# A transformer decoder layer on one core: the order of the first loads, masks and transposes

## The chip, the cores and the metric

The kernel runs on one core of a Trainium2 chip. The core has a matrix engine (PE), a vector engine (DVE), a scalar engine for activation functions (ACT), a general engine (POOL) and a queue engine (SP), which work side by side and meet through semaphores. Transfers between the chip's memory and the on-chip buffers are issued by SP, ACT and POOL and carried by 16 DMA engines that all three share. The metric is the device time of one execution in microseconds, lower is better.

## The reference

The computation is one post-norm decoder layer on x of 16 x 256 tokens with 256 features, in float32: a "quantum" self-attention, a differential cross-attention over a context, and a mixture of four experts, each followed by a layer norm. Only the beginning of the first attention matters here:

```python
Q = (x @ wq + bq).reshape(Bn, Sn, Hn, hd)      # 16 heads of 16 features; K with wk, bk, V with wv, bv
def prep(t):
    h1 = jnp.tanh(jnp.einsum('bshd,do->bsho', t, w1) + b1)     # 16 -> 256 for each head
    return jnp.einsum('bsho,on->bshn', h1, w2) + b2            # 256 -> 16
qp, kp = (prep(Q), prep(K))
q1 = jnp.einsum('bshn,nm->bshm', qc, Hc)        # qc, kc: complex pairs of the 16; Hc: the 8 x 8 hadamard
...                                             # rotations by rot, squared norms qq and kk
attn = jax.nn.softmax(s / s, axis=2)            # s = qq * kk
out = jnp.einsum('bijh,bjhd->bihd', attn, V).reshape(Bn, Sn, Dn)
return out @ wo + bo
```

Since everything from w2 to the Hadamard matrix is linear, the kernel multiplies the second layer's weights (and b2) by the Hadamard matrix once, at the start.

## The kernel before, in words

Tokens are worked in 8 pairs of sequences, 512 tokens each, q = 0 to 7. For a pair, `turn_x` (line 801) transposes two halves of features of x on PE, four 128 x 128 blocks into one PSUM bank, and DVE copies the bank out as xT. `project` (811) multiplies xT with wk or wq into `pq`; DVE adds the bias into qT. `hidden(t)` (830) is one of 16 steps of a pair: four matmuls of 32 rows (`ph`), two heads' first layers, with w1 taken from a tile `w1p` that holds w1 eight times, once per head, masked for even and odd heads; ACT takes tanh of the two results (`h`). `outer` (845) multiplies `h` with the second layer's weights `w2p` into `pe`. All `mm` calls share line 119 in the profile.

The first lines of `first_attention` (777) issue the loads: wk on SP, then on ACT's queue the eight copies of w1 (783), bk, b1 and rot; wq, wv, wo on SP; bq on ACT; x of the pairs 1 to 7 on SP. Before them x of pair 0 was issued on SP. After the function definitions come, in program order, the two `turn_x` of pair 0 and its first `project` (1001 to 1003), the head masks on POOL (`mask8`), their sum `mpar` on DVE (1010), the two products that mask `w1p` (1013), further masks on POOL, and then the loads of w2T, b2 and the 8 x 8 Hadamard matrix on ACT (1043 to 1053). That matrix is put twice on the diagonal of `hb1`, a 16 x 16 tile that DVE clears first; DVE also clears `w2p`. `second_layer` (1056), planned for step 0, multiplies w2T by hb1 (`pw`), copies the result into `w2p`, and multiplies b2 by an expanded copy of hb1 (`hbd`) into the bias `b2c`.

Each engine runs its instructions in program order: for PE, ACT and DVE the order is that of the code (`ORDERED`, line 27), which the plan's steps write out (line 1125: `hidden(t)` first, then planned work, then `outer` of the step before). A DMA is issued at its place in the order of the engine that issues it. SP's and ACT's transfers use eight completion counters in rotation, in the order in which both queues are laid out; a transfer whose counter was used before is issued only after that earlier transfer has landed. PSUM banks for `ptx`, `pq` and `pw` come from `bank` (798), a pool tagged `sm` with one buffer, so that each use waits until the one before was read; `pe` has a bank of its own in the pool `pse`, not used before the first `outer`.

Of the kernel before, what the change touches and what calls it, by code (L numbers as in the profile page):

```python
# [9 lines left out]
F32 = mybir.dt.float32  # L10
# [5 lines left out]
P = 128  # L16
B, S, D = 16, 256, 256
# [46 lines left out]
def bc(ap, axis, n):  # L64

    shape = list(ap.shape)
    return ap.unsqueeze(axis).to_broadcast(shape[:axis] + [n] + shape[axis:])
# [3 lines left out]
def decoder_kernel(ctx: ExitStack, tc: tile.TileContext, a: dict, out: bass.AP):  # L71
    nc = tc.nc
    PE, DVE, ACT, POOL, SP = nc.tensor, nc.vector, nc.scalar, nc.gpsimd, nc.sync
# [17 lines left out]
    def mat(pool, key, n, eng=SP):  # L91

        k = a[key].shape[0]
        t = pool.tile([P, k // P, n], F32, tag=key, name=key)
        eng.dma_start(out=t, in_=a[key].rearrange("(c p) f -> p c f", p=P))
        return t

    def col(pool, key, eng=SP):

        n = a[key].shape[0]  # L100
        t = pool.tile([P, n // P], F32, tag=key, name=key)
        eng.dma_start(out=t, in_=a[key].rearrange("(c p) -> p c", p=P))
        return t
# [14 lines left out]
    def mm(out_, lhsT, rhs, start=True, stop=True):  # L118
        PE.matmul(out=out_, lhsT=lhsT, rhs=rhs, start=start, stop=stop)  # L119
# [648 lines left out]
    hd = heads.enter_context(tc.tile_pool(name="hd", bufs=1))  # L768
    ps = heads.enter_context(tc.tile_pool(name="psA", bufs=1, space=PSUM))
    pse = heads.enter_context(tc.tile_pool(name="psAe", bufs=1, space=PSUM))  # L770
    psb = heads.enter_context(tc.tile_pool(name="psAb", bufs=3, space=PSUM))
    wH = folds.enter_context(tc.tile_pool(name="wH", bufs=1, side="right"))
# [4 lines left out]
    def first_attention():  # L777

        plan = Plan()
        wk = mat(hd, "L0_attn_wk", D)  # L780
        w1p = hd.tile([P, 2, D], F32, tag="w1p", name="w1p")
        for k in range(8):
            ACT.dma_start(out=w1p[16 * k:16 * k + 16, 1, :], in_=a["L0_attn_w1"])
        bk, b1 = (col(hd, f"L0_attn_{n}", ACT) for n in ("bk", "b1"))
        rot = wH.tile([H, NQ, 3], F32, tag="rot", name="rot")
        ACT.dma_start(out=rot, in_=a["L0_attn_rot"])
        wq, wv = (mat(hd, f"L0_attn_{n}", D) for n in ("wq", "wv"))
# [10 lines left out]
        def bank(name):  # L798
            return banks[0].tile([P, 512], F32, tag="sm", name=name)

        def turn_x(q, c):
            xq = xs[:, q * CPB:(q + 1) * CPB, :]
            xT = xTs[q, c] = hd.tile([P, TB], F32, tag="xT", name="xT", bufs=4)
            pt = bank("ptx")
            for n in range(CPB):
                PE.transpose(pt[:, n * P:(n + 1) * P], xq[:, n, c * P:(c + 1) * P], ident)
            DVE.tensor_copy(xT, pt)
            if c == 1:
                POOL.tensor_tensor(xq, xq, bc(bo, 1, CPB), ALU.add)

        def project(q, side, cc):
            w, bias = ((wk, bk), (wq, bq))[side]
            qT = qTs[q, side, cc] = hd.tile([P, TB], F32, tag="qT", name=f"qT{q}{side}", bufs=2)
            pq = bank("pq")
            for c in range(2):
                mm(pq, w[:, c, cc * P:(cc + 1) * P], xTs[q, c], c == 0, c == 1)
            DVE.tensor_scalar(qT, pq, bias[:, cc:cc + 1], None, ALU.add)
# [180 lines left out]
            DVE.tensor_tensor(xv, pf.rearrange("p (i d) -> p i d", i=2), xv, ALU.add)  # L998
            plan.later(1, norm, n0)

        for c in range(2):
            turn_x(0, c)
        project(0, 0, 0)

        mask8 = hd.tile([P, 8], F32, tag="mask8", name="mask8")
        POOL.memset(mask8, 1.0)
        POOL.affine_select(mask8, mask8, [[-16, 8]], ALU.is_ge, 0.0, base=0, channel_multiplier=1)
# [3 lines left out]

        for par in range(2):
            DVE.tensor_scalar(w1p[:, par, :], w1p[:, 1, :], mpar[:, par:par + 1], None, ALU.mult)

        b16 = tl.tile([P, H], F32, tag="b16", name="b16")
        POOL.memset(b16, 1.0)
# [23 lines left out]
                DVE.tensor_copy(selc[:, cc, 8 * cc:8 * cc + 8], b8)  # L1040


        w2T = wH.tile([16, D], F32, tag="w2T", name="w2T")
        ACT.dma_start(out=w2T, in_=a["L0_attn_w2T"])
        b2 = wH.tile([16, 1], F32, tag="b2", name="b2")
        ACT.dma_start(out=b2, in_=a["L0_attn_b2"].unsqueeze(1))
        hbd = wH.tile([16, 8, 16], F32, tag="hbd", name="hbd")
        hb1 = wH.tile([16, 16], F32, tag="hb1", name="hb1")
        DVE.memset(hb1, 0.0)
        for k in range(2):  # L1050
            ACT.dma_start(out=hb1[8 * k:8 * k + 8, 8 * k:8 * k + 8], in_=a["L0_attn_hadamard"])
        w2p = hd.tile([P, 2, 2, 32], F32, tag="w2p", name="w2p")
        DVE.memset(w2p, 0.0)
        b2c = hd.tile([P, 1], F32, tag="b2c", name="b2c")

        def second_layer():
# [54 lines left out]
        for q in range(NPAIR):  # L1111
            s0 = 16 * q
            for c in range(2):
                if q:
                    plan.job(s0 - 6, s0 - 4 + c, turn_x, q, c)
            for side in range(2):
                for cc in range(2):
                    f = s0 + 8 * side + 4 * cc
                    if f:
                        plan.job(f - 3, f - 1, project, q, side, cc)  # L1120
            for half in range(2):
                plan.job(*((s0 + 15, s0 + 24 + half) if q < NPAIR - 1 else (LAST - 2, 0)), values, q, half)
# [362 lines left out]
    with ExitStack() as own:  # L1485
        own.enter_context(tc.manual_schedule(engines=ORDERED))
        planA, stepA, fold = first_attention()
        xw, xb, tri, mw, mb, rb = ffn_small()
        zero = tl.tile([P, P], F32, tag="zero", name="zero")
# [100 lines left out]
```

## Time and profile before

| | us |
|---|---|
| median of 3 runs (lowest, highest) | 1847.62 (1845.48, 1850.51) |
| profiled execution | 1848.87 |
| its span, first to last instruction | 1846.9 |
| PE busy in 0 to 28 us | 12.08 |
| PE busy in 28 to 60 us | 30.23 |
| PE busy in 60 to 100 us | 40.00 |

A line of the profile names the engine, the source line, the operation, and its output and inputs with the program's tile names, from which digits are dropped: `hb` is hb1, `b` is b2 or b16 according to its line, and `L_attn_b` of line 102 is b1. "ACTq" and "SPq" stand for the time in which an engine issues a transfer. The brackets give how long the engine had been idle and what ended that. Where an engine spends its time in issuing transfers, which isn't counted as busy, a wait is put down to the transfer that came last.

### The profile page before, as it was taken

What the parts mean: (1) busy time and instruction counts of PE and PEld (TensorE: products, weight loads), DVE (VectorE), ACT (ScalarE), POOL (GpSimd) and SP (SyncE); (2) the same over time, 40 slices, a digit from 0 to 9 for tenths busy, and PEclk for the clock granted to TensorE, in tenths of its full rate; (3) what the DMA queues carried; (4) which work ended last, traced back from release to release, by engine and by line L of the source; (5) the groups of instructions that cost most, each with busy time, mean ns of one, the idle gap of its engine ahead of it and who ended that gap; (6) DMA issues with size and microseconds to landing.
All of it is one profiled execution on the core that took longest, in us unless ns stands there. A gap on an engine that the chain in (4) does not pass through costs nothing. (4 is left out here: it accounts for less than half of the span.)

```text
span 1846.9 us, 32370 instructions
## 1 busy us (share of the span) xinstructions
PE 1682.0 (91%) x12254; PEld 960.4 (52%) x12254; DVE 960.4 (52%) x2033; ACT 942.6 (51%) x1368; POOL 536.5 (29%) x1235
## 2 busy tenths in 40 slices
PE   6999999999999999999999999997987999899743
PEld 2343434343444656656565655564664758566533
DVE  1225656655556876777766666672213334121565
ACT  3547777777777576665655556554322222231210
POOL 5001313212313333344634343445320110131331
PEclk9999999999999999999999999898998999899876
DMA  9912111212112200000101000011333001221322
GB/s 258 297 50 70 65 59 59 69 59 93 58 59 98 65 14 14 3 25 14 37 2 36 2 25 2 25 37 47 102 103 109 20 28 48 82 75 39 106 64 81
DMA packets 117771, 115.34 MB, mean 62 GB/s; under 512 B 7776, under 2 KB 111408, under 8 KB 117584
## 3 DMA queue, kind: packets, MB, share of 16 engines
q1 hardware_dynamic: 108560, 93.08, 15.8%
q0 software_dynamic: 7824, 19.65, 3.6%
q8 instruction: 114, 1.87, 0.4%
q14 instruction: 73, 0.60, 0.1%
q10 hardware_dynamic: 1200, 0.15, 0.1%
HBM read 73.79 MB, written 38.54 MB: 61 GB/s over the span
## 5 line engine op out<-in xcount | busy, mean ns | idle before, releaser
L1307 DVE TENSOR_REDUCE mpad<-p 128x4 f32<-128x1024 f32 x256 | 311.3, 1218 | 142.3 <-PE p L119 141.4
L1313 ACT ACTIVATE e<-p 128x512 f32<-128x512 f32 x512 | 276.7, 596 | 175.5 <-PE p L119 173.7
L841 ACT ACTIVATE h<-ph,L_attn_b 128x1024 f32<-128x1024 f32 x256 | 271.3, 1112 | 160.9 <-PE ph L119 160.9
L119 PE MATMUL p<-qp,kT 32*128 32x256 f32 x2048 | 315.3, 410 | 18.2 <-DVE o L1360 13.3
L119 PE MATMUL p<-kT,qp 32*128 32x256 f32 x2048 | 314.1, 409 | 1.5 <-DVE mpad L1307 1.5
L119 PEld LDWEIGHTS p<-kT,qp 32*128 32x128 f32 x2048 | 193.7, 188 | 91.0 <-issue 49.7
L119 PEld LDWEIGHTS p<-qp,kT 32*128 32x128 f32 x2048 | 207.9, 190 | 31.7 <-issue 25.6
L119 PE MATMUL ph<-qT,w1p 32*128 32x512 f32 x1024 | 152.3, 652 | 3.1 <-ACT h L841 1.8
L935 DVE TENSOR_TENSOR z<-rqb,ra 128x1024 f32<-128x1024 f32 x120 | 151.5, 1265 | 3.7 <-DMA rqb<-rqd 1.7
L119 PE MATMUL pe<-h,w2p 128*32 128x512 f32 x1024 | 138.2, 612 | 1.6 <-DVE enc L858 0.9
L119 PE MATMUL pob<-e,vaug 128*32 128x512 f32 x1024 | 128.3, 620 | 0.0
L942 ACT ACTIVATE z<-z 128x1024 f32<-128x1024 f32 x120 | 127.1, 1060 | 1.3 <-DVE z L935 0.9
L628 POOL DMA_INDIRECT ya<-xlist,place x64 | 62.8, 981 | 205.0 <-DVE xs L638 86.7
L159 POOL TENSOR_SCALAR ln_ve<-ln_mv 128x2 f32<-128x2 f32 x32 | 7.2, 225 | 351.3 <-DVE ln_mv L157 350.5
L119 PE MATMUL pw<-xeT,L_ffn_sw_w 128*128 128x512 f32 (+1 forms) x256 | 85.8, 496 | 12.8 <-DVE xeT L478 12.8
L163 POOL TENSOR_SCALAR xs<-xs,ln_mv,rs_y 128x256 f32<-128x256 f32 x64 | 83.8, 1314 | 3.4
L478 ACT ACT_TABLE_LOAD x17 | 21.8, 1283 | 113.7 <-PE pt L477 113.3
L119 PE MATMUL po<-z,vaug 128*32 128x256 f32 x1024 | 72.8, 389 | 6.7 <-DVE ra L895 1.6
L119 PEld LDWEIGHTS pw<-xeT,L_ffn_sw_w 128*128 128x128 f32 x256 | 50.0, 196 | 47.1 <-issue 28.7
L404 POOL DMA_INDIRECT xlist<-xs,place x64 | 62.7, 980 | 37.1 <-DVE place L401 19.7
L119 PEld LDWEIGHTS ph<-qT,w1p 32*128 32x128 f32 x1024 | 42.5, 184 | 53.8 <-issue 42.0
L1339 ACT COPY ovTb<-pob 128x512 f32<-128x512 f32 x64 | 37.5, 585 | 58.2 <-PE pob L119 58.2
(349 smaller groups left out, 2598.1 us busy)
## 6 DMA issues: line engine op xcount, KB each, us to landing
rqb<-rqd SPq DMA_DIRECT2D x64, 512.0 KB
xlist<-zero SPq DMA_DIRECT2D x16, 1024.0 KB
xe<-xlist SPq DMA_DIRECT2D x21, 512.0 KB
xlist<-ye SPq DMA_DIRECT2D x14, 512.0 KB
xs<-in_x SPq DMA_DIRECT2D x8, 512.0 KB
cx<-in_ctx SPq DMA_DIRECT2D x8, 512.0 KB
qp<-st SPq DMA_DIRECT2D x256, 2.0 KB
out<-xs SPq DMA_DIRECT2D x8, 512.0 KB
```

Of the source, the lines that this page charges most:

```text
L119: PE.matmul(out=out_, lhsT=lhsT, rhs=rhs, start=start, stop=stop)
L159: POOL.tensor_scalar(ve, mv[:, :, 1], EPS, None, ALU.add)
L163: POOL.tensor_scalar(x, x, mv[:, i, 0:1], r[:, i:i + 1], ALU.subtract, ALU.mult)
L404: put = POOL.indirect_dma_start(xlist[g][:], bass.IndirectOffsetOnAxis(ap=place[:, n, k:k + 1], axis=0), xs[:, q * CPB + n, :], None)
L478: (DVE.tensor_copy if c else ACT.copy)(t[:, c, :n * P], pt[:, :n * P])
L628: POOL.indirect_dma_start(t[:, n, :], None, xlist[group(q)][:], bass.IndirectOffsetOnAxis(ap=moe["place"][:, q * CPB + n, k:k + 1], axis=0),)
L841: ACT.activation(h, phs[gp], AF.Tanh, bias=b1[:, fc:fc + 1])
L935: DVE.tensor_tensor(z, bc(rqbs[u][:, 2 * gp:2 * gp + 2], 2, 2), bc(rk, 3, S), ALU.mult)
L942: ACT.activation(z, z, AF.Exp)
L1307: DVE.tensor_reduce(mpads[j % 2][:, 2 * gp:2 * gp + 2, :, ic], p1, AX.X, ALU.max, negate=True)
L1313: ACT.activation(e[:, gi], p2[gi], AF.Exp)
L1339: ACT.copy(o, po)
```

## The change

Four edits, all in `first_attention`. The tiles w2T, b2, hbd, hb1 and w2p are made at the top, and the two clearing operations on DVE stand ahead of every load. The two loads of the Hadamard matrix, w2T and b2 are issued on ACT right behind w1, bk and b1, and ahead of rot and bq. The masks, `mpar` and the products that mask `w1p` come before the transposes of x and the first projection. Of the two transposes of pair 0 the second uses the bank of `pe` in place of the `sm` bank.

```diff
         w1p = hd.tile([P, 2, D], F32, tag="w1p", name="w1p")
+        w2T = wH.tile([16, D], F32, tag="w2T", name="w2T")
+        b2 = wH.tile([16, 1], F32, tag="b2", name="b2")
+        hbd = wH.tile([16, 8, 16], F32, tag="hbd", name="hbd")
+        hb1 = wH.tile([16, 16], F32, tag="hb1", name="hb1")
+        w2p = hd.tile([P, 2, 2, 32], F32, tag="w2p", name="w2p")
+        DVE.memset(hb1, 0.0)
+        DVE.memset(w2p, 0.0)
         for k in range(8):
             ACT.dma_start(out=w1p[16 * k:16 * k + 16, 1, :], in_=a["L0_attn_w1"])
         bk, b1 = (col(hd, f"L0_attn_{n}", ACT) for n in ("bk", "b1"))
+        for k in range(2):
+            ACT.dma_start(out=hb1[8 * k:8 * k + 8, 8 * k:8 * k + 8], in_=a["L0_attn_hadamard"])
+        ACT.dma_start(out=w2T, in_=a["L0_attn_w2T"])
+        ACT.dma_start(out=b2, in_=a["L0_attn_b2"].unsqueeze(1))
         rot = wH.tile([H, NQ, 3], F32, tag="rot", name="rot")
...
-            pt = bank("ptx")
+            pt = pse.tile([P, 512], F32, tag="pe", name="ptx") if (q, c) == (0, 1) else bank("ptx")
...
-        for c in range(2):
-            turn_x(0, c)
-        project(0, 0, 0)
-
         mask8 = hd.tile([P, 8], F32, tag="mask8", name="mask8")
...
         for par in range(2):
             DVE.tensor_scalar(w1p[:, par, :], w1p[:, 1, :], mpar[:, par:par + 1], None, ALU.mult)
+
+        for c in range(2):
+            turn_x(0, c)
+        project(0, 0, 0)
...
-        w2T = wH.tile([16, D], F32, tag="w2T", name="w2T")
-        ACT.dma_start(out=w2T, in_=a["L0_attn_w2T"])
-        b2 = wH.tile([16, 1], F32, tag="b2", name="b2")
-        ACT.dma_start(out=b2, in_=a["L0_attn_b2"].unsqueeze(1))
-        hbd = wH.tile([16, 8, 16], F32, tag="hbd", name="hbd")
-        hb1 = wH.tile([16, 16], F32, tag="hb1", name="hb1")
-        DVE.memset(hb1, 0.0)
-        for k in range(2):
-            ACT.dma_start(out=hb1[8 * k:8 * k + 8, 8 * k:8 * k + 8], in_=a["L0_attn_hadamard"])
-        w2p = hd.tile([P, 2, 2, 32], F32, tag="w2p", name="w2p")
-        DVE.memset(w2p, 0.0)
         b2c = hd.tile([P, 1], F32, tag="b2c", name="b2c")
```

## The prediction

> **What bounds the kernel now.** First the page's totals, for the engine that sets the length:
>
> ```profile
> span 1846.9 us, 32370 instructions
> PE 1682.0 (91%) x12254; PEld 960.4 (52%) x12254; DVE 960.4 (52%) x2033; ACT 942.6 (51%) x1368; POOL 536.5 (29%) x1235
> ```
>
> TensorE (PE) is busy for 91% of the span. Busy time by stage puts the gaps at the two ends: 12.08 us of PE work in the first 28 us, then 30.23 of 32, then 40.00 of 40. The change touches only the opening, so the question is which wait ends last there. The timeline of the opening, PE alone (start, duration, operation; in brackets the idle time before and what ended it):
>
> ```profile
> 6.85 1.12 PE L806 MATMUL ptx<-ident,xs 128*128 128x128 f32 x4 [0.78 <-DVE xT L807]
> 8.75 3.78 PE L119 MATMUL pq<-xT,L_attn_wk 128*128 128x512 f32 x4 [0.78 <-DVE xT L807]
> 13.83 2.09 PE L119 MATMUL ph<-qT,w1p 32*128 32x512 f32 x8 [1.30 <-DVE w1p L1013]
> 23.30 0.57 PE L119 MATMUL pw<-hb,w2T 16*128 16x16 f32 x2 [7.38 <-DMA hb<-in_L_attn_hadamard]
> 24.22 0.61 PE L119 MATMUL pw<-hb,w2T 16*128 16x16 f32 x2 [0.35 <-DVE w2p L1062]
> 25.17 0.37 PE L119 MATMUL pw<-b,hbd 16*128 16x1 f32 x1 [0.35 <-DVE w2p L1062]
> 25.19 1.23 PE L119 MATMUL ph<-qT,w1p 32*128 32x512 f32 x3
> 25.41 0.35 PE L119 MATMUL pw<-b,hbd 16*128 16x1 f32 x1
> 25.62 2.05 PE L119 MATMUL ph<-qT,w1p 32*128 32x512 f32 x5
> 27.60 1.94 PE L119 MATMUL pe<-h,w2p 128*32 128x512 f32 x8
> ```
>
> The longest gap is 7.38 us ahead of the second-layer product (`pw<-hb,w2T`), and it ends with the landing of the Hadamard matrix. Everything of the next step (`ph` at 25.19) is queued behind it on PE. Why the matrix is late shows on ScalarE's timeline, with its DMA queue (ACTq):
>
> ```profile
> 8.00 0.48 ACTq L786 DMA_DIRECT2D rot<-in_L_attn_rot  x1
> 8.52 0.44 ACTq L102 DMA_DIRECT2D L_attn_bq<-in_L_attn_bq  x1
> 9.00 0.80 ACTq L1044 DMA_DIRECT2D w2T<-in_L_attn_w2T  x1
> 12.74 0.34 ACTq L1046 DMA_DIRECT2D b<-in_L_attn_b  x1
> 15.36 1.65 ACTq L1051 DMA_DIRECT2D hb<-in_L_attn_hadamard  x2
> 17.09 1.28 ACT L841 ACT_TABLE_LOAD   x1 [17.09 <-DMA b<-in_L_attn_b]
> 18.39 2.12 ACT L841 ACTIVATE h<-ph,L_attn_b 128x1024 f32<-128x1024 f32 x2
> 27.74 2.12 ACT L841 ACTIVATE h<-ph,L_attn_b 128x1024 f32<-128x1024 f32 x2 [7.24 <-PE ph L119]
> ```
>
> Names drop digits: `b` of L1046 is b2, `hb` is hb1. SP and ACT share eight completion counters in rotation, and a transfer may be issued only when the last one on its counter has landed. b2 waits so for wo (landed 12.72 by the trace's completion events). hb1 waits for w2T (landed 15.28); that, not the memset of 14.23, is why it starts at 15.36. Its two halves land at 22.28 and 23.16. They also hold ScalarE: the table load at 17.09 stands behind them. Last, DVE's order, where the mask work comes after the projection:
>
> ```profile
> 8.00 0.69 DVE L807 COPY xT<-ptx 128x512 f32<-128x512 f32 x1 [1.21 <-PE ptx L806]
> 12.57 0.75 DVE L817 TENSOR_SCALAR qT<-pq,L_attn_bk 128x512 f32<-128x512 f32 x1 [3.88 <-PE pq L119]
> 13.23 0.15 DVE L1010 TENSOR_REDUCE mpar<-mask 128x2 f32<-128x8 f32 x1
> 13.42 0.86 DVE L1013 TENSOR_SCALAR w1p<-w1p,mpar 128x256 f32<-128x256 f32 x2
> ```
>
> [...] ACT's bk, b1, rot, bq, w2T land in issue order at 12.22, 13.06, 14.34, 14.73, 15.28, each 5.4 to 6.3 us after issue, while x tiles stream beside them. [...] the eight `pe` matmuls take 1.94 us at 27.60 and 1.06 at 33.66.
>
> **The change part by part**, on the profiled execution.
>
> 1. Order of DVE. mpar and the two w1p products move ahead of the xT copies. They wait for all eight w1 loads; the last landed at 8.98. So w1p runs 9.02 to 9.88 (0.86). The xT copies, whose banks are full at 6.07 and (transposes now back to back, no 0.78 gap) about 7.2, run only 9.88 to 10.57 and to 11.28. The second bank thus buys nothing, both copies being late; were w1 in by 6 us, it would save the 0.78. pq starts after the first copy (in the built program its two matmuls now wait for one copy each) at 10.63, plus 3.78 is 14.41; the second copy is there at 11.28, before the first half of pq ends. qT 14.45 to 15.20, ph 15.24. Before, ph began at 13.83: **+1.41 us**.
> 2. Hadamard and w2T. The order on ACTq becomes w1, bk, b1, hb1, hb2, w2T, b2, rot, bq. hb1 and hb2 now follow, on their counters, the sixth and seventh w1 load (landed 7.75 and 7.92), so they take the places of rot and bq at 8.00 and 8.52; the memset they need runs near 1 us, DVE having nothing else before 4. In those places rot and bq landed at 14.34 and 14.73, and w2T, in its old place, at 15.28. ph ends at 15.24 + 2.09 = 17.33, so pw starts at 17.36 without a wait: **-7.35 us** (7.38 - 0.03).
> 3. b2 keeps its place behind wo, 12.74, and landed at 19.36. PE reaches its matmul 25.17 - 23.30 = 1.87 after pw, at 19.23. If b2 lands as before the cost is 0.13. It may land earlier: x3, issued at 12.23 just ahead of it, now waits for x1 (14.53). Latest bound: behind a transfer as slow as x3 (10.6 us from issue to landing), 23.4, cost 4.2. I take 0, since w2T went from issue to landing in 6.3 and b2 is smaller.
> 4. rot and bq go out at about 13.1 and 13.55. With the 6.6 us of b2 they land by 20.2; rot is used at 33.36 - 5.9 = 27.5, bq at 46.4 - 5.9. Nothing. The ACT queue is free at 13.99, the table load ends at 15.28, ahead of tanh at 17.3: hidden. If it were not, 1.28.
> 5. x3 to x7 go out up to 2.3 us later (counters now follow x1, hb1, hb2, w2T, x2), and f1w, ce_gen_w and the zero fill follow b2, rot, bq. x1 keeps its place, landed 14.53 and is turned at 64. The others are read much later. Nothing. POOL's addition to x starts at 7.3 instead of 8.06, its DMAs keep their time since the first of them now follows the addition: nothing.
>
> Sum: 1.41 - 7.35 = -5.94 us. From pw to the third tanh it is 27.74 - 23.30 = 4.44, so that tanh starts at 21.8. Does it last? All PE waits between 28 and 110 us:
>
> ```profile
> PE ph L119 <- ACT h L841: 1.8, 1, 1.8
> ```
>
> That one is at 39.95, behind ScalarE's sine tables, which move along. Transfers with fixed times have room: me_wo landed at 28.4 and is used at 54.6, me_c1w 50.0 and 67.4. So it is carried to the end: span 1841.0, profiled execution 1848.87 - 5.9 = 1843.0. The median of the runs shown, 1847.62, is 1.25 lower: **1841.7 us**.
>
> **Rivals.** Within 0.3% (5.5 us) is about what a measurement of this kernel can tell from no change; my gain is barely above it.
>
> - A, as worked out: 1841.7, own range 1840.3 to 1842.6. Chance 0.60, of which 0.51 gains over 5.5.
> - B, b2 takes the place of the Hadamard wait, at L119 `pw<-b,hbd`. For it: 19.36 against 19.23, no room. Against: fewer x bytes ahead. At 21.3 the gain is 3.9: 1843.8. Chance 0.17.
> - C, the earlier issue is worth little: hb or w2T still lands near 20 to 22 us, because the DMA engines are full (hb took 6.9 us from issue to landing at 15.36), or a later wait eats the gain. Against it: in the same places of the queue rot, bq and w2T landed by 15.28, and the list of PE waits above is short. Gain 1 to 3: about 1845.6. Chance 0.10. That the transfers don't move at all is excluded by the built order.
> - E, PE is released to full clock earlier. Before, `pe` and `pq` of 27.6 to 32.6 ran slow: 1.94 + 3.19 against 1.06 + 1.98 warm, 2.1 at most. PE now works from 15.2 with short gaps. 1839.6. Chance 0.08. [...]
> - D, slower: the w1 loads at the head of DVE. The copies of x, ready at 6 to 7, now stand behind them, and through pq, qT and ph everything else; each us later costs one. Landed at 8.98 they leave 5.94, so from 14.9 on the change loses, and from 20.5 it is slower by over 0.3%. If the last of them took the 14.3 us of x5 (14.55 to 28.85) instead of 2.5, it would land at 20.8 and cost 5.9: 1853.5. Against it: nothing that is issued ahead of them is changed. Chance 0.05.
>
> **How the numbers follow.** Faster: 0.51 of A, 0.08 of E, 0.03 of B, 0.62. Same: 0.09 + 0.14 + 0.10 = 0.33. Slower: D, 0.05. The range holds A, B, E and half of C: 1838.5 to 1846.0[...].
>
> **What would show it.** Right: w1p at 9.0 on DVE ahead of both xT copies; pq near 10.6; ph near 15.2; pw near 17.4 with no DMA wait; third tanh near 21.8; rows after 28 us shifted by 5 to 7 and no new PE wait. Wrong: a DMA wait before either pw (B or C), w1p later than 9.5 (D), or a new gap later in the opening.

## The result, and the profile after

The changed kernel takes 1843.92 us (median of 21 runs, 1841.69 to 1847.74); the kernel before, run beside it, 1847.60 (21 runs, 1844.38 to 1858.09). The ratio is 0.9976 with a 95% interval of 0.9968 to 0.9985, or 4.4 us (2.8 to 5.9); the two medians lie 3.7 us apart. It is a small gain, inside the 0.3% that the prediction treated as no difference and below its 5.9 us. The median lies inside the stated range (1838.5 to 1846.0) and above the own range of rival A (1840.3 to 1842.6). The profiled execution took 1844.83 us. All ratios leave out executions in a slower state of the chip, of which these runs have one, at 2780.59 us in e5_step1.

The page's totals of the kernel after, to be held against those of before:

```profile
span 1843.1 us, 32365 instructions
PE 1684.0 (91%) x12254; PEld 960.8 (52%) x12254; DVE 961.2 (52%) x2033; ACT 942.6 (51%) x1368; POOL 537.3 (29%) x1235
```

PE has the same 12254 instructions, but is 2.0 us longer at them: part of what the waits gave back was spent at a slower clock (0.955 of full speed on average, 0.958 before). PE's timeline of the opening, after (start, duration, operation; in brackets the idle time before and what ended it):

```profile
4.91 1.94 PE L817 MATMUL ptx<-ident,xs 128*128 128x128 f32 x8 [4.91 <-POOL rep L1033]
11.81 3.78 PE L119 MATMUL pq<-xT,L_attn_wk 128*128 128x512 f32 x4 [4.96 <-DVE xT L818]
16.44 2.09 PE L119 MATMUL ph<-qT,w1p 32*128 32x512 f32 x8 [0.84 <-DVE qT L828]
18.31 0.44 PE L119 MATMUL pw<-hb,w2T 16*128 16x16 f32 x2
...
20.05 0.37 PE L119 MATMUL pw<-b,hbd 16*128 16x1 f32 x1 [0.35 <-DVE w2p L1062]
...
24.35 2.13 PE L119 MATMUL pq<-xT,L_attn_wk 128*128 128x512 f32 x4
...
33.83 1.13 PE L119 MATMUL ph<-qT,w1p 32*128 32x512 f32 x6 [1.77 <-ACT h L852]
34.90 1.93 PE L119 MATMUL pe<-h,w2p 128*32 128x512 f32 x8
```

The wait of 7.38 us ahead of `pw<-hb,w2T` is gone. In its place stands a wait of 4.96 us ahead of `pq`, for the copies of x, behind which everything is later than forecast: `ph` at 16.44, not 15.24. The last two lines show a second loss. The wait of 1.77 us behind the sine tables was there before, at 39.95, and was followed by a `pe` of 1.07 us; now the `pe` after it takes 1.93. In the profile of before:

```profile
39.95 1.13 PE L119 MATMUL ph<-qT,w1p 32*128 32x512 f32 x6 [1.77 <-ACT h L841]
41.02 1.07 PE L119 MATMUL pe<-h,w2p 128*32 128x512 f32 x8
```

ScalarE and its queue, after:

```profile
8.22 0.96 ACTq L793 DMA_DIRECT2D hb<-in_L_attn_hadamard  x2
9.22 0.32 ACTq L794 DMA_DIRECT2D w2T<-in_L_attn_w2T  x1
...
18.58 2.12 ACT L852 ACTIVATE h<-ph,L_attn_b 128x1024 f32<-128x1024 f32 x2 [4.75 <-PE ph L119]
22.62 2.12 ACT L852 ACTIVATE h<-ph,L_attn_b 128x1024 f32<-128x1024 f32 x2 [1.92 <-PE ph L119]
```

The Hadamard matrix is issued 7.1 us earlier and is there at 12.7, w2T at 13.3 (by the completion events). The third tanh, the last line, starts 5.12 us earlier than before. Next DVE, after, and the one addition that POOL runs beside it:

```profile
4.08 0.16 DVE L1017 TENSOR_REDUCE mpar<-mask 128x2 f32<-128x8 f32 x1 [2.98 <-POOL mask L1015]
9.37 1.79 DVE L1020 TENSOR_SCALAR w1p<-w1p,mpar 128x256 f32<-128x256 f32 x2 [5.13 <-DMA hb<-in_L_attn_hadamard]
11.09 1.27 DVE L818 COPY xT<-ptx 128x512 f32<-128x512 f32 x2
```

```profile
7.98 2.34 POOL L820 TENSOR_TENSOR xs<-xs,L_attn_bo_bc 128x1024 f32<-128x1024 f32 x1 [0.87 <-issue]
```

Masking `w1p` took 0.86 us before, now 1.79. (Its bracket names the Hadamard matrix, which landed only at 12.5; what it waits for are the w1 loads, the last of them landed at 9.05.) Last, PE's clock: stretches cut at the clock's own steps, after and then before. The columns are the stretch, its length, busy time of PE, PEld, DVE, ACT and POOL, the granted PE clock, DMA share and GB/s.

```profile
24.70:31.50 6.80, 6.80 (x38) 1.99 (x37) 2.95 (x13) 3.78 (x6) 5.78 (x9) 1.00 1.08 361
31.50:34.90 3.40, 1.63 (x9) 0.31 (x7) 0.00 (x0) 3.27 (x3) 2.00 (x4) 1.00 0.87 206
34.90:38.30 3.40, 3.40 (x19) 1.04 (x17) 0.75 (x1) 2.12 (x2) 0.00 (x0) 0.50 0.92 161
38.30:45.00 6.70, 6.70 (x44) 2.34 (x39) 2.31 (x10) 4.24 (x4) 0.00 (x0) 1.00 1.13 338
```

```profile
35.30:38.70 3.40, 2.88 (x18) 0.46 (x12) 0.17 (x2) 3.35 (x4) 0.00 (x0) 1.00 0.97 219
38.70:42.10 3.40, 2.15 (x15) 0.55 (x15) 0.00 (x0) 3.10 (x4) 0.00 (x0) 1.00 1.13 343
```

The recorded steps of the clock lie whole windows of 3.41 us apart (after: 24.68, 34.92 and 38.34, so 3 windows and 1; before: 31.92, 120.67 and 124.08, so 26 and 1). A border at which the clock does not step is not recorded; its place is worked out from the steps. After, the wait of 1.77 us falls whole into the window from 31.5, and the next window runs at half clock (0.50). Before, the wait lay across two windows (0.57 us in the first, 1.21 in the second), and the clock stayed at 1.00.

So the gain goes like this, as the start of each tanh against the same tanh before: third -5.12, fifth -6.12, the one that began at 47.58 before -4.72, and still -4.73 at 97 us. From there to the end the difference swings between about -6.4 and -1.4 with single half-clock windows that fall at different times in the two kernels (at 120.7 us before, at 188.5 after, for example) and ends at -3.8 in the span. The stretch up to 100 us lies ahead of these windows and is the sharper measure; "shift" below is that of the tanh which began at 47.58 us before. It has a scatter of its own, since the clock moves the opening too: three profiles of the changed kernel gave -4.72, -6.63 and -5.14. A difference of under 2 us between two single profiles is therefore no evidence by itself.

### The profile page after: what moved, and what is told of

It is laid out like the page before. It is cut to its first block, busy times and chain, and to the rows that moved or that the text cites. A ratio compares the mean times of both kernels' runs of the same rounds, so it can differ in the third digit from the quotient of the medians.

```text
span 1843.1 us, 32365 instructions
## 1 busy us (share of the span) xinstructions
PE 1684.0 (91%) x12254; PEld 960.8 (52%) x12254; DVE 961.2 (52%) x2033; ACT 942.6 (51%) x1368; POOL 537.3 (29%) x1235
## 5 line engine op out<-in xcount | busy, mean ns | idle before, releaser
L119 PEld LDWEIGHTS p<-qp,kT 32*128 32x128 f32 x2048 | 207.3, 189 | 31.5 <-issue 25.7
L478 ACT ACT_TABLE_LOAD x17 | 21.8, 1283 | 113.7 <-PE pt L477 113.3
```

What stands on the lines that cost most here:

```text
L478: (DVE.tensor_copy if c else ACT.copy)(t[:, c, :n * P], pt[:, :n * P])
```

## The experiments

My theory after this comparison: the early loads make the gain; the new order of DVE costs more than forecast, since `w1p` runs beside POOL's addition; and a half-clock window after the sine tables takes 1.4 us back. The first rival has the order and the second bank as the gain; the second, that the DMA landings move with any reordering and nothing can be put down to one edit.

The twelve runs fall in three groups, each on one chip, with the kernel before run beside it: 1879.90, 1848.13 and 1848.77 us. Ratios and shifts are compared, not times: on record the first and the third group even have the same chip number, so that the 31 us between them stay unexplained. The shift is against the one profile of before, that of the sections above; the first group parts from it only after 714 us, where the same differences grow by 7.5 to 8.8 us up to 831 us in all four of its runs (and by 27 to 31 us to the end).

| run | what it is | shift, us | ratio (95% interval) |
|---|---|---|---|
| e1_loads | early loads and clearing alone | -8.54 | 0.9964 (0.9950, 0.9977) |
| e2_masks | masks ahead of the projection alone | +0.61 | 1.0001 (0.9984, 1.0018) |
| e3_late_add | whole change, POOL's addition later | -7.73 | 0.9974 (0.9961, 0.9988) |
| after_again | whole change | -6.63 | 0.9977 (0.9965, 0.9988) |
| e4_loads_banks | e1_loads and the second bank | -8.43 | 0.9964 (0.9951, 0.9977) |
| e5_step1 | e1_loads, second layer at step 1 | -3.85 | 0.9983 (0.9976, 0.9990) |
| e6_all | whole change and five edits | -8.36 | 0.9964 (0.9950, 0.9978) |
| e7_sine | e6_all, sines ahead of the first tanh | -10.36 | 0.9940 (0.9927, 0.9953) |
| e8_sine0 | whole change, sines at step 0 | -10.85 | 0.9956 (0.9943, 0.9970) |
| e9_loads_sine | e1_loads, sines at step 0 | -11.74 | 0.9944 (0.9931, 0.9958) |
| e5_again | e5_step1, a second profile | -5.76 | one run |
| after_third | whole change, a third profile | -5.14 | one run |

### Half of the change at a time

**e1_loads** keeps the first half of the diff, and leaves the order of transposes, projection and masks, and the single bank, as before:

```diff
-            pt = pse.tile([P, 512], F32, tag="pe", name="ptx") if (q, c) == (0, 1) else bank("ptx")
+            pt = bank("ptx")
...
+        for c in range(2):
+            turn_x(0, c)
+        project(0, 0, 0)
+
         mask8 = hd.tile([P, 8], F32, tag="mask8", name="mask8")
...
-        for c in range(2):
-            turn_x(0, c)
-        project(0, 0, 0)
```

> The early clearing and the early loads alone: the projection before the masks and one bank for both transposes, as in the kernel before. My theory: the whole gain is the Hadamard matrix, w2T and b2 landing early, and the masks put ahead of the projection only cost. Then w1p runs at 13.4 for 0.86 us after qT, ph starts at 13.8, pw at 15.9 with no DMA wait, the third tanh at 20.3 (27.74 before, 22.62 with the whole change), and the time is 7 us below the kernel before, 2 to 2.5 below the whole change. Rival: the new order or the second bank carries part of the gain; then the third tanh is at 22.6 or later. Rival: b2 lands late here since PE asks for it 2.6 us sooner; then a DMA wait stands before the b2 product at 17.7.

**e2_masks** is the other part of it, from the kernel before: only the calls of `turn_x` and `project` move behind the products that mask `w1p`; loads and bank stay.

```diff
-        for c in range(2):
-            turn_x(0, c)
-        project(0, 0, 0)
-
         mask8 = hd.tile([P, 8], F32, tag="mask8", name="mask8")
...
             DVE.tensor_scalar(w1p[:, par, :], w1p[:, 1, :], mpar[:, par:par + 1], None, ALU.mult)
+
+        for c in range(2):
+            turn_x(0, c)
+        project(0, 0, 0)
```

> The masks and the w1p products ahead of the projection, and nothing else of the change. My theory: ph moves from 13.8 to about 16.4, but that is covered, since PE still waits for the Hadamard matrix until 23.3; third tanh at 27.7, time as before within 1 us. Rival: the new order helps in itself; then the third tanh is earlier than 27 and the time 1.5 us or more below before.

The early loads alone have the whole gain and more: shift -8.54, where the change has -4.7 to -6.6, and the third tanh at 19.46 (20.3 was expected). PE's timeline of e1_loads:

```profile
13.88 1.14 PE L119 MATMUL ph<-qT,w1p 32*128 32x512 f32 x8 [1.30 <-DVE w1p L1024]
15.34 0.36 PE L119 MATMUL pw<-hb,w2T 16*128 16x16 f32 x2 [0.32 <-DMA w2T<-in_L_attn_w2T]
```

`ph` is at 13.88, as before the change, against 16.44 after it, and what is left of the 7.38 us wait is 0.32. The order alone (e2_masks) gives nothing: its `pw` still waits for the Hadamard matrix, which is issued at 16.88 there and landed at 23.8.

```profile
23.95 0.58 PE L119 MATMUL pw<-hb,w2T 16*128 16x16 f32 x2 [5.93 <-DMA hb<-in_L_attn_hadamard]
```

The first rival falls. Of the second, so much is true that landings move: w2T landed at 13.29, 14.26 and 15.46 in three profiles of the changed kernel. But in all twelve profiles with the early loads the matrix and w2T were there between 12.4 and 15.6 us, and in the two without them the matrix came at 23.2 and 23.8. By the medians the order takes 0.13% from the early loads, but the two intervals overlap; what separates them is the start of `ph` in the traces.

### What the order costs, and why

**e3_late_add** is the whole change with POOL's addition of the bias bo to pair 0 put off to step 3; **after_again** is the changed kernel beside it.

```diff
-            if c == 1:
+            if c == 1 and q:
...
+        def later_add():
+            xq = xs[:, :CPB, :]
+            POOL.tensor_tensor(xq, xq, bc(bo, 1, CPB), ALU.add)
+
+        plan.at(3, later_add)
```

> The whole change, with POOL's addition of bo to the first pair's x moved from 8.0 us to step 3. My theory: the two w1p products took 1.79 us in place of 0.86 because POOL's addition ran at the same time[...]. Then they take 0.86 here, the copies of xT begin 0.9 us earlier (10.2 in place of 11.1), ph at 15.5, third tanh at 21.7, time about 1 us below the whole change. Rival: they are slow for another reason (DMA writes into the on-chip memory, or the loads of w1 just before); then they stay near 1.8 us and nothing moves.

> The whole change once more, for the phase of PE's clock. My theory: until the third tanh all positions repeat within 0.3 us (22.6), while the speed of the first pe and pq groups and of the pe group after ScalarE's sine tables (1.93 us at 34.9, against 1.06 warm) changes from execution to execution by up to 1.4 us. Rival: the cold stretch at 34.9 comes from the change itself (an earlier and so longer gap); then it repeats here.

The masking of `w1p` in e3_late_add:

```profile
9.19 0.83 DVE L1020 TENSOR_SCALAR w1p<-w1p,mpar 128x256 f32<-128x256 f32 x2 [4.94 <-DMA hb<-in_L_attn_hadamard]
```

0.83 us without the addition, 1.66 with it in after_again (1.79 and 2.28 in the other two profiles of the changed kernel). The first of the two products started at 9.37, 9.45 and 8.87 in the three profiles and took 1.10, 0.96 and 1.59 us, so it ended at 10.47, 10.40 and 10.46: each time 0.15 us or a little less behind the end of POOL's addition (10.32, 10.26 and 10.31). In e8_sine0, further down, the two products took 1.55 us. Alone, in e3_late_add and before the change, one takes 0.35 to 0.47. The end of the first product follows that of the addition: a product that starts 0.5 to 0.6 us earlier ends at the same time, once the addition is over. It ends only 0.15 us after it, less than the 0.35 that it takes alone, so that it was not held back for its whole time. What the two engines compete for, the traces do not show. The second copy of xT, which reads PSUM, ran beside the same addition before the change (8.00 and 8.06) at 0.69 us, as long as the first, which had no addition beside it. That the second product also takes 0.66 us is not explained: POOL issues a transfer then, but it does so in e3_late_add too, where the second product takes 0.35.

`ph` comes at 13.88 (e1_loads), 15.07 (e3_late_add) and 16.37 (after_again): 1.19 us go with the order, and 1.30 lie between the kernels without and with the addition. Of these, 0.83 are the longer products; their later start (9.45 instead of 9.19) and a `pq` that was granted full clock later (3.78 us instead of 3.56) make up the rest. The third tanh comes at 19.46, 19.98 and 20.96, so 1.5 of the 2.5 us reach it; in e1_loads, ScalarE's table load ends at 15.1 and `pw` waits for w2T until 15.3 anyway. The ratios can't tell e3_late_add (0.9974) from after_again (0.9977), so the cost of the addition rests on the traces. The third tanh missed both expectations, 21.7 for e3_late_add and 22.6 for after_again: in both, the clock was granted earlier than in the first profile of the changed kernel, at 13.9 and 15.7 us instead of 24.7.

### The second bank

**e4_loads_banks** gives e1_loads the second bank:

```diff
-            pt = bank("ptx")
+            pt = pse.tile([P, 512], F32, tag="pe", name="ptx") if (q, c) == (0, 1) else bank("ptx")
```

> The early loads and clearing, with the old order of the projection ahead of the masks, and the second transpose of pair 0 in a bank of its own. Compared with the run that has the early loads and one bank (w1p at 13.47, ph 13.88, pw 15.34, third tanh 19.46). My theory: with DVE free when the banks fill, the 0.78 us gap between the transposes goes, the second xT copy ends near 7.2 instead of 8.7, and pq starts near 7.0 to 7.2; but bk lands at 10.2 to 12.2, so qT, ph and w1p are gated by a landing and not by pq, ScalarE's first tanh stands behind the issue of bq and the table load (about 15.1), and pw behind w2T's landing (about 15.2). So third tanh within 0.5 us of 19.46, time within 1 us of the early loads alone (ratio 0.996 to 0.997). Rival: the bank passes its 0.8 to 1.8 us on, third tanh at 17.7 to 18.7, ratio near 0.9955.

`pq` starts at 7.32 instead of 8.80 and `ph` at 11.75 instead of 13.88, but `pw` waits for w2T until 15.36 and the third tanh is at 19.37 against 19.46: with the old order the bank is worth nothing, as expected, since a landing sets the end. One expectation in it missed: the first tanh was not held to 15.1 but ran at 13.17, because bq went out at 11.45. With the new order the bank does count: e2_masks, which has one bank, starts `pq` at 12.26, and e3_late_add with two at 10.67, both without an addition beside `w1p`.

### Moving more out of the way, and the clock

**e5_step1** plans the second layer for step 1 on top of e1_loads, so that PE does the next `ph` before `pw`:

```diff
-        plan.at(0, second_layer)
+        plan.at(1, second_layer)
```

> The early loads alone, with the second layer's product planned for step 1 instead of step 0, so that PE does ph of step 1 before pw. My theory: with the loads early, what sets the third tanh of 19.46 is pw behind w2T (15.2) and the ph that is queued behind pw. With ph of step 1 ahead of pw, the third tanh follows the first two at once, near 17.3, and the opening is shorter by 1.5 to 2.2 us more: shift after 45 us near -10. Rival: PE has the same work to do in the same time and was only waiting for 0.3 us there, so the shift stays at -8.5 within 0.6.

> The early loads with the second layer at step 1, a second look. If its half-clock windows (16 to 26 and 33 to 40 us) belong to the kernel's own gaps, they stand at the same places within a window of 3.4 us and the shift after 45 us is near -3.9 again; if they belong to the chance phase of the clock's windows in one execution, the shift after 45 us can be anything from -4 to -8.

The third tanh came at 18.34, 1.1 us earlier than in e1_loads, and yet the shift is -3.85 instead of -8.54; by the ratio the gain is smaller too, 0.17% against 0.36%. The third tanh is no measure any more, since part of the second layer's work now comes behind its `ph`: the first `pe` starts at 20.20, in e1_loads at 19.32. PE's clock in e5_step1, columns as above:

```profile
15.90:26.10 10.20, 9.10 (x28) 3.28 (x32) 0.88 (x6) 3.39 (x4) 3.65 (x9) 0.50 0.91 259
26.10:32.90 6.80, 5.47 (x34) 1.32 (x30) 2.80 (x13) 5.62 (x6) 6.74 (x11) 1.00 1.11 344
32.90:39.70 6.80, 6.36 (x28) 2.09 (x32) 0.90 (x2) 3.79 (x5) 0.43 (x1) 0.50 0.99 236
```

Five windows at half clock, where e1_loads has two (16.2 to 23.0). Between 16 and 20.2 us PE waits three times for a tanh or a copy (0.35 to 0.44 us each), and gets full clock back 3.1 us later than in e1_loads (26.1 against 23.0), so that `pq` takes 3.78 us instead of 2.89; behind the sine wait the clock closes again. The second profile has the same shape with other places (half clock until 24.1 and from 34.3 to 37.7, shift -5.76), which speaks for a chance phase of the clock's windows. The theory and the rival that were set down for e5_step1 both missed, since neither had the clock in it.

**e6_all** is the whole change with five edits more:

```diff
-        ACT.dma_start(out=rot, in_=a["L0_attn_rot"])
+        POOL.dma_start(out=rot, in_=a["L0_attn_rot"])
...
-        bq = col(hd, "L0_attn_bq", ACT)
+        bq = col(hd, "L0_attn_bq", POOL)
...
-            if c == 1:
+            if c == 1 and q:
...
+        for c in range(2):
+            turn_x(0, c)
+
         mask8 = hd.tile([P, 8], F32, tag="mask8", name="mask8")
...
             DVE.tensor_scalar(w1p[:, par, :], w1p[:, 1, :], mpar[:, par:par + 1], None, ALU.mult)
 
-        for c in range(2):
-            turn_x(0, c)
         project(0, 0, 0)
...
-        plan.at(0, second_layer)
+        plan.at(1, second_layer)
...
+        plan.at(3, later_add)
```

> The whole change with five edits more: the products that mask w1 stand between the two xT copies and qT (so transposes do not wait for w1), POOL's first addition of bo to step 3, second layer at step 1, rot and bq on POOL's queue. My theory: xT copies near 6.9 and 7.3, pq near 7.0 to 7.3, w1p at about 9 to 9.5 for 0.85, qT 11 to 12.5 (bk's landing), ph about 11.6 to 13, table load at 11 to 12 instead of 12.5 to 13.8, first tanh near 13.5 (b1's landing), third tanh 15.5 to 17, shift after 45 us of -10 to -11.5, ratio near 0.9945. Rival: what was saved is eaten by another landing (w2T, bq or x1), then it stays within 1 us of the early loads alone.

The third tanh is at 16.85, within the expectation, and the shift only -8.36, as in e1_loads. Of the 2.6 us by which the third tanh was earlier, 0.6 are left at the first `pe` (18.71 against 19.32), because the work of `pw` comes behind `ph` here and PE waits 0.95 us for the first tanh; and `pq` behind it, nearly all of it at half clock, took 3.66 us instead of 2.89, which ate these. At the next `ph` the two kernels are level (24.17 and 24.00). The rival, another landing, is not seen.

**e7_sine** takes the sine tables out of the middle: the function `angles`, otherwise unchanged, is defined and called behind the two `turn_x` and ahead of the masks, and its place at step 2 is dropped.

```diff
         for c in range(2):
             turn_x(0, c)
 
+        angles()
+
         mask8 = hd.tile([P, 8], F32, tag="mask8", name="mask8")
...
-        plan.at(2, angles)
```

> As the run before (all five edits), and the angles and the two sine lookups of the rotations stand ahead of the first tanh instead of at step 2. My theory: PE's wait of 1.8 us for tanh that follows the sine tables (34 to 40 us) goes, and with it the slow pe matmuls of 1.93 us after it[...]; the sine tables cost the first tanh nothing if rot lands by 12, and up to 3 us if it lands later than b1. No PE wait over 1 us between 20 and 110 us, pe at 1.06 to 1.07 throughout, shift after 45 us -12 to -13. Rival: rot lands at 14 or later and the first tanh is held as long as the stall was: shift no better than in the run before.

No PE wait is left between 20 and 110 us, and the shift is 2.0 better than e6_all: the 1.77 us of the wait and 0.2. It is less than the -12 to -13 that was forecast, since e6_all had no half-clock window behind its sine wait that could have been saved.

**e8_sine0** and **e9_loads_sine** test this with one line, on the changed kernel and on e1_loads:

```diff
-        plan.at(2, angles)
+        plan.at(0, angles)
```

> The whole change, and with it the angles and the two sine lookups planned for step 0 instead of step 2, so that they stand behind the first two tanh. It takes away PE's 1.77 us wait after 32 us, nothing else on PE. My theory: the half-clock window of 3.4 us that follows this wait in the changed kernel (34.9 to 38.3) is caused by the wait; then it goes too, and the shift after 45 us is -8 (the changed kernel's -4.7, less 1.77, less 1.4 to 1.6), third tanh near 24 but off PE's path. The time falls by about 3 us, ratio about 0.996. Rival: the half-clock window falls in the same place whatever PE does before it: the shift is -6.5 at most, and PE's clock is 0.5 somewhere between 30 and 42 us all the same.

> The early loads and clearing alone (masks and transposes in the old order, one bank), with the sine lookups at step 0 instead of step 2. My theory: the early loads gave a shift of -8.5 with no half-clock window after the sine wait, so that only the wait's 1.77 us is to be had: -10.3, ratio about 0.9945, as good as the run with all six edits. Rival: DVE's angles and ScalarE's tables at step 0 hold up the next tanh or qT by as much as they save: shift -8.5 again.

> The changed kernel again, a third look. If the half-clock window after the sine wait belongs to the kernel, it is there a third time (pe near 34 at 1.93, shift after 45 us between -4.7 and -6.7); if it is chance, a third of such looks or more should be without it, as 6 of 8 looks at the other kernels with this wait were, and the shift is then near -8 with pe at 1.06.

PE's clock in e8_sine0, in the stretch where the changed kernel was slow:

```profile
31.40:34.80 3.40, 3.40 (x21) 1.46 (x21) 2.22 (x10) 3.12 (x4) 1.70 (x3) 1.00 1.13 311
34.80:38.20 3.40, 3.40 (x23) 1.06 (x25) 0.75 (x1) 1.53 (x3) 0.00 (x0) 1.00 0.93 170
```

With the wait gone the half-clock window is gone too, in all three kernels without it (e7_sine, e8_sine0, e9_loads_sine); with it, the changed kernel had one in all three profiles (34.9, 32.7 and 34.1 us). (Where the expectation of after_third has six of eight profiles of other kernels without the window, it is five.) Once full clock had come to stay, no profile of the fourteen has a half-clock window before 45 us but behind this wait, and the six whose clock was read on to 100 us (before, after and e4_loads_banks to e7_sine) were granted 1.00 from 60 to 100 us. So the window after 32 us is caused by the wait, though the wait does not always bring it. The shift of e8_sine0 is 6.1 better than that of the changed kernel's first profile, more than the 1.77 and 1.4 that go; most of the rest I put down to the clock, which this execution was granted at 15.1 us instead of 24.7, with one slow window at 18.5; that part is argued, not shown. e9_loads_sine, the early loads and one line, takes 1839.31 us against 1848.77 of the kernel before and e7_sine 1838.21 against 1848.13, a gain of 0.56% (0.42 to 0.69) and 0.60% (0.47 to 0.73) where the change had 0.24% (0.15 to 0.32). The ratios of e8_sine0 and e9_loads_sine are close to the 0.996 and 0.9945 expected. e9_loads_sine and e7_sine beat both kernels; between them, and e8_sine0, the runs do not decide.

## Why the prediction was right, and where it was not

**Direction and main mechanism: right.** Step 2, hb1, hb2 and w2T in the places of rot and bq: `pw` has no DMA wait, and e1_loads shows that this edit carries the gain. The matrix landed at 12.5 to 12.7, and w2T at 13.3, earlier than the 14.3 to 15.3 of the places that they took over; in the third profile they came at 15.3 and 15.5, still ahead of their use.

**Step 1, order of DVE: right in kind, mis-sized.** `w1p` ran ahead of both copies and everything stood behind it. The forecast was 9.02 for 0.86 us; measured 9.37 for 1.79. Of the 0.35 us, 0.07 is the last w1 load (9.05 instead of 8.98); then three semaphore instructions of 50 ns stand at 9.1 to 9.3 ahead of the first product. The 0.93 us go with POOL's addition, which step 5 called "nothing": without it, in e3_late_add, the products took 0.83. It runs at 7.98, hardly earlier than the 8.06 of before and not at the forecast 7.3. Its cost on DVE was not asked for, though either start, with its 2.34 us, puts it over the forecast time of `w1p`. `ph` came 1.20 us later than forecast for it, the third tanh 0.82 (22.62 against 21.8).

**"The second bank thus buys nothing": wrong as a statement, without effect on the sum.** The working already used two full banks. With one bank the second transpose would have waited for the late first copy; e2_masks against e3_late_add puts that at 1.6 us of `pq`. In e4_loads_banks, where DVE is free, it put `pq` 1.5 us forward as well, and the landing of w2T took that back.

**Step 3, b2 at no cost: right.** `pw<-b,hbd` at 20.05 waits for DVE alone; b2 landed at 14.40, 5 us earlier than before: it went out 2.1 us earlier, when wo had landed (10.59 instead of 12.72), and took 3.8 us instead of 6.6, with x3 now issued behind it. That was the mild side of the stated uncertainty, and rival B falls with it.

**Step 4, rot, bq and the table load hidden: right.** The table load ran from 12.54 to 13.8, bq landed at 17.66, and no PE wait but the known one is left after 24 us. **Step 5, later x and weights: right; its POOL addition: wrong**, as above.

**Carried to the end: right on the whole, with two clock terms that cancel only in part.** Rival E did happen beside A: full clock was granted at 24.7 instead of 31.9, and the `pq` at 24.35 took 2.13 us instead of 3.19, 1.0 us gained. Then the half-clock window at 34.9 cost 1.40. The working of the prediction did not see that the known wait at 39.95, moved by 6 us, would lie differently in the clock's windows. The three terms close the account of this profile: 0.82 - 1.00 + 1.40 = 1.22 us, which is 5.94 less 4.72. How these two clock terms fall out changed from profile to profile: after_again, the same kernel, stood at -6.63.

**Rivals C and D** fall by the landings (hb1 12.5, last w1 9.05). D's mechanism, the head of DVE, is nevertheless where the missing microsecond is; its price came with POOL's addition and not from a late w1.

**The chances.** 0.62 went to a gain over 0.3%; the measured 0.24% (0.15 to 0.32) is in the case that got 0.33. The forecast gain of 5.9 us lay only 0.4 above that border, so costs of a microsecond, which it had not priced, decided it.

## To carry to other kernels

When an instruction is moved to a time at which another engine is busy, look at what that engine does then: an addition on POOL that had cost nothing for as long as it ran beside a PSUM copy (0.69 us, as without it) doubled the time of two VectorE products that read and write SBUF (0.83 us without it, 1.66 to 2.28 beside it). A wait that a change doesn't touch can still change its price: here the clock closed behind it all five times that the wait of 1.77 us fell whole into one of the clock's windows of 3.41, and once in six times when it was split. So after the waits, read the granted clock of each stretch, and where a stall is known and its work can go elsewhere (here one line for the sine tables), take it out rather than shift it.

## What the runs showed of the hardware

**A wait of 1.77 us was enough for half clock.** That is 52% of a window of 3.41 us, the unit in which the recorded steps of the clock lie apart. In eleven profiles PE has that same wait. In the five where it lies whole in one window (the three of the changed kernel, e2_masks, e5_again) the next window was at half clock. In the six where a border splits it (before 0.57 and 1.21, e1_loads 0.21 and 1.56, e3_late_add 0.49 and 1.28, e4_loads_banks 0.40 and 1.37, e6_all 1.00 and 0.77, e5_step1 1.35 and 0.42) it stayed at full clock, but for e5_step1. As an estimate from 1.77 and 3.41, a wait that starts anywhere in a window with equal chance lies whole in it in 48% of the cases; it did so in five of eleven.

**PE's idle time alone sets no border.** In six openings a window at full clock was followed by half clock though PE was idle in it for only 1.26 to 1.54 us in all (e6_all from 10.3 us 1.26, e7_sine from 10.9 1.27, e5_step1 from 12.4 1.31, after_again from 15.7 1.39, e3_late_add from 13.9 1.41, e8_sine0 from 15.1 1.54), less than the 1.56 us after which e1_loads stayed open. The half-clock window of before at 120.7 us even follows a window in which PE had no idle time (117.26 to 120.67, busy for 3.41 of 3.41 us at a granted clock of 1.00). What else decides was not tried and stays open.

**The same kernel starts at different clocks.** The three profiles of the changed kernel were first granted full clock at 24.7, 15.7 and 23.8 us, and their third tanh ran at 22.62, 20.96 and 22.61. One profile's opening is good to some 1.7 us, which is as much as the effects of single edits here.
